# Attention and GraphSAGE of one kernel put into one fixed order, with common PSUM banks and tiles, and the first GraphSAGE batch prepared in the last attention steps

## The chip, the cores and the metric

The kernel runs on one core of a Trainium2 chip. Its engines run side by side: TensorE (PE, whose weight loads are listed apart as PEld), VectorE (DVE), ScalarE (ACT), GpSimd (POOL) and SyncE (SP), which here only issues transfers. A DMA transfer is started by an instruction on an engine's queue and lands on its own; the engines meet through semaphores. Times are device microseconds (us) of one execution. The time of the kernel before is the median of three runs, 3646.37 us (3645.41 to 3649.14).

## What is computed

Two graph layers over B = 16 graphs of N = 1024 nodes with D = 128 features and a dense adjacency with values 0 or 0.05 to 1. All data are float32.

```python
# layer 0: attention with H = 8 heads of 16
h = relu(layernorm(x))
q, k, v = (h @ W.T + b split into heads)
attn = softmax(where(adj == 0, -inf, q @ k.T / 4)) * adj
attn = attn / (attn.sum(-1) + 1e-8)
x = x + (attn @ v) @ Wo.T + bo

# layer 1: GraphSAGE on a thinned adjacency
h = relu(layernorm(x))
for n in range(1024):                  # one after the other, in each graph
    # of row n's remaining neighbours every sf-th is removed, from row and column
    sf = (num + 1) // 2 if num > 10 else 1
adj_d = adj * kept
for Wr, Wx, b, g, be in three layers:
    deg = max(adj_d.sum(-1), 1)
    out = (adj_d @ h) / deg @ Wr + h @ Wx + b
    h = batch_norm(relu(out / max(norm(out), 1e-12) * mask))   # statistics over all graphs and nodes
x = x + ((concat(h1, h2, h3) * mask) @ Wl + bl) * mask
```

## The kernel before

**Attention** is a chain of 512 half-steps: for each batch b (16), each half c of the 512 query rows (2), each block m of 128 keys (8), each group g of four heads (2). One half-step computes on PE the scores of four heads into two tiles `sc` (L459 puts a large negative number where there is no edge, L465 adds q times k), on ACT their exponentials `e` (L481), on DVE the product `w` with the transposed adjacency (L486), and on PE the sums over w and e into `acc` (L383, L388), one half-step later (`late`). Even half-steps also transpose a piece of the adjacency (L414) that ACT copies to `aT` (L417); that is stored to DRAM (`aT_d`) for GraphSAGE. L421 makes `nomask`, which also counts zeros.

Beside these steps run others, written as generators and taken on in a list `beside`. `go_on_with(kinds)` advances the first whose next part is of a wanted kind: True is a PE part, "evict" and "evict by VectorE" are the copies out of PSUM, False is work that needs neither. `prepare(b + 1)` makes q, k and v of the next batch, from `xt` with a layer norm (statistics on DVE, a power on POOL at L235, the normalisation on ACT at L241). `conclude` (L311 to L357) finishes a half of a batch: divide by the sums (L329 to L333, with a copy of the reciprocals to `rden` on POOL), transpose (L337), multiply by Wo (L347), add to x (L352); after the second half it also stores x (L355), makes the layer norm for GraphSAGE and stores its result `h0_d` (L357).

**The dilation** is a third generator, run beside attention by `beside_attention`: eight blocks of 128 rows over all 16 graphs, whose parts carry a cost, and which is advanced so that the sum of the costs keeps pace with the half-steps (`spent < total * (i + 16) / n_att`). It writes `mr_d`, nonzero where an edge was removed. Its last block ends shortly before attention does; two half-steps later the loads for GraphSAGE's first two turns are issued by `edges` (L122 to L131): the transposed adjacency of a half batch (2 MB) and two pieces of `mr` (512 KB each). Issued by name from ACT's queue, they stand among ACT's own instructions.

The order of PE, ACT and DVE in attention is the order of the code, since all of it is under `tc.manual_schedule`. The queues of SP and POOL are ordered by the scheduler of the tile framework.

**Between the two.** After the last half-step (L499) the second half of batch 15 is concluded, with nothing beside it. L826 to L843 add up what must hold for the sweep to be valid (`still`, `pf`, `bad`) into `flag`; a second form of the kernel, `walked`, runs if that is not zero, which it is not for these inputs. Then the masks of turn 0 are applied (L139: four pieces of 128 x 1024 per turn, an edge is dropped where mr is not zero); in the order that the scheduler builds, these and those of turn 1 stand on DVE among the last attention products. The attention pools, SBUF and PSUM, close here, and the pools const2, p2, p2small and p2ps take their memory: six weights, wl and bl (L857 to L862), norms, `ys` with a column of ones by memset (L877), rdeg, hTs.

**GraphSAGE** is 3 layers x 16 batches x 2 halves, 96 turns, again under `tc.manual_schedule`. Before each layer `incoming` and `given` prepare batch 0: in the first layer h0 is loaded (L931, from POOL's queue) and transposed (L939, L940), then multiplied by Wr into `ys` (L949, L950); a batch later on is prepared beside the one before. A turn (`nodes`) is: own = bias + h Wx (L105, L963), copied by ACT to `mine` (L966); sums over 8 x 4 blocks of the masked adjacency into `pg` (L971), in four parts with other work between them; degrees (L978, L981); o = pg / degree + mine (L985); its square (L990) and norm (L993 to L999), relu and scale (L1000); transposes (L1004), a copy into hTs (L1005) and statistics (L1007). The second part of one turn, from the square on, is run between the parts of the next turn's sums, as are the four mask pieces of the turn after. The adjacency is loaded three turns ahead, from SP's queue (`fetch`, L1012 to L1014). From the second layer on, `output_part` (L893) adds the layer's share of the output.

[...]Attention's tags are sc (2 tiles of 2 banks), acc0, acc1, m, d; GraphSAGE's are g (2 tiles of 2 banks), n, o, t, y.

Of the kernel before, what the change touches and what calls it, by code (L numbers as in the profile page):

```python
# [34 lines left out]
def swept(ctx: ExitStack, tc: tile.TileContext, t: dict, out: bass.AP, flag: bass.AP):  # L35
# [108 lines left out]

    ahead = {}

    with ExitStack() as p1:
# [3 lines left out]
        ps_s = p1.enter_context(tc.tile_pool(name="ps_s", bufs=2, space=PSUM))  # L151
        ps_o = p1.enter_context(tc.tile_pool(name="ps_o", bufs=1, space=PSUM))
        ps_m = p1.enter_context(tc.tile_pool(name="ps_m", bufs=1, space=PSUM))
        ps_d = p1.enter_context(tc.tile_pool(name="ps_d", bufs=1, space=PSUM))
# [3 lines left out]
        def load_x(b):  # L158
            if b < B:
                xts[b] = pool.tile([P, NB, D], F32, name=f"xt_{b}", tag="xin", bufs=3)  # L160
                nc.sync.dma_start(xts[b], x[b].rearrange("(k p) d -> p k d", p=P))
# [4 lines left out]
        nr_i = small.tile([B * NB, P], I32, name="nr_i", bufs=1)  # L166
        nc.sync.dma_start(nr_i, nodemask.rearrange("b (k p) -> (b k) p", p=P))
        nr_f = small.tile([B * NB, P], F32, name="nr_f", tag="raw", bufs=1)
# [3 lines left out]
        nc.vector.tensor_copy(mf, mps[:, : B * NB])  # L172
        nc.vector.tensor_scalar(
# [5 lines left out]
        raw = pool.tile([P, 4, D], F32, name="raw", tag="s", bufs=1)  # L179
# [39 lines left out]
        minus_half = one.tile([P, NB], F32, name="minus_half")  # L219
        nc.vector.memset(minus_half, -0.5)  # L220

        def layer_norm_relu(dst, src, name):

            st = small.tile([P, NB, 6], F32, name=f"st_{name}", tag="lnst", bufs=2)
            mv = small.tile([P, NB, 2], F32, name=f"mv_{name}", tag="lnmv", bufs=2)
# [7 lines left out]
            rs = small.tile([P, 2, NB], F32, name=f"rs_{name}", tag="lnrs", bufs=2)  # L233
# [11 lines left out]
        def prepare(b):  # L245
# [4 lines left out]
            h = pool.tile([P, NB, D], F32, name=f"h_{b}", tag="s", bufs=1)  # L250
            yield from layer_norm_relu(h, xt, f"a{b}")
            hT = one.tile([P, N], F32, name=f"hT_{b}", tag="hT")
# [105 lines left out]

        ready = {}
# [16 lines left out]
        def attention():  # L376
# [62 lines left out]
            for i, (b, c, m) in enumerate(turns):  # L439
                mm = slice(m * P, (m + 1) * P)  # L440
                if m == 0:
# [3 lines left out]
                    if c == 0 and b + 1 < B:  # L445
                        take_on(prepare(b + 1), len(beside))
                if c == 1 and m == HB + 1:
                    load_x(b + 2)
# [51 lines left out]
            take_on(conclude(*done), 0)  # L500
            while beside:
                go_on_with(True, False, "evict", "evict by VectorE", "first")
# [18 lines left out]
        def dilation():  # L521
# [23 lines left out]
            def fetch(k, b):  # L545

                ad = pool.tile([P, N], F32, name=f"ad_{k}_{b}", tag="ad", bufs=2)
# [1155 lines left out]
```

## Time and profile before

| | us |
|---|---|
| median of three runs (lowest, highest) | 3646.37 (3645.41, 3649.14) |
| the profiled execution's own time | 3647.81 |
| its span, first to last instruction | 3645.9 |
| PE busy | 3447.8 (95%) |
| DVE busy | 3161.1 (87%) |
| ACT busy | 2300.6 (63%) |
| POOL busy | 155.5 (4%) |
| PE, sums `pg` (L971) | 737.9, 6144 of 275 ns on average |
| PE, sums `acc` (L383 and L388) | 651.0 and 625.0, 4096 each |
| DVE, product `w` (L486) | 1204.3, 1024 of 1217 ns |
| DVE, masks (L139) | 458.8, 384 of 1217 ns |
| ACT, exponentials (L481) | 990.6, 1024 of 1020 ns |

The profile is of one execution. Busy times of an engine are shares of the whole span; a row of it cuts the span into 40 slices of 91 us with one digit each (tenths of the slice in which the engine was busy), and a row PEclk gives TensorE's granted clock in the same way. A window gives busy times in a stretch. In a timeline a line is: start (us from the start of the span), duration, engine, line of the code, operation, out<-in, shapes, how many were joined into the line, and in brackets how long the engine was idle before and what ended it. ACTq, SPq and POOLq are transfers issued on the queue of that engine. The chain of waits goes back from the last instruction to what released it.

### The profile page before, as it was taken

The page shows a single profiled execution, that of the slowest core. Times are in us where ns is not written, and L with a number is a line of the kernel's source. Part 1 is how long each engine was busy: PE and PEld are TensorE (multiplying, and loading weights), DVE is VectorE, ACT ScalarE, POOL GpSimd, SP SyncE. Part 2 cuts the span into 40 slices and gives each one's busy share as a digit, 9 for nine tenths or more (in the row PEclk, how much of TensorE's full clock was granted, in tenths as well). Part 3 has the DMA queues.
Part 4 walks back from the last instruction along what each step waited for, and adds up shares of the span by engine and source line. Part 5 has one row for each costly group of instructions (what it writes and reads, how often), then busy time and mean ns, then how long its engine had stood idle before and what let it go on. Part 6 is the DMA issues. An engine that isn't in the chain of part 4 may idle for free. (4 is left out here: it accounts for less than half of the span.)

```text
span 3645.9 us, 86038 instructions
## 1 busy us (share of the span) xinstructions
PE 3447.8 (95%) x34855; PEld 1895.4 (52%) x34855; DVE 3161.1 (87%) x5215; ACT 2300.6 (63%) x3813; POOL 155.5 (4%) x210
## 2 busy tenths in 40 slices
PE   6999999999999999999999999977999899989997
PEld 2333333333333333333333333326999799989996
DVE  3999999999989999999999999974788688878786
ACT  5689679779769869868967876852222333322224
POOL 1000000000000000000000000000000000000000
PEclk9999999999999999999999999988999999999999
DMA  6346447547637636736845853666999788889996
GB/s 189 112 143 198 148 118 215 150 124 217 179 110 212 200 115 199 222 109 184 238 138 151 233 169 109 188 208 225 329 331 318 257 318 314 317 298 333 332 332 197
DMA packets 654305, 772.77 MB, mean 212 GB/s; under 512 B 173765, under 2 KB 574026, under 8 KB 641610
## 3 DMA queue, kind: packets, MB, share of 16 engines
q1 hardware_dynamic: 639978, 718.95, 61.4%
q0 software_dynamic: 11520, 41.95, 3.3%
q8 instruction: 275, 4.51, 0.5%
q10 hardware_dynamic: 2400, 6.29, 0.5%
q14 instruction: 132, 1.08, 0.1%
HBM read 509.02 MB, written 157.29 MB: 183 GB/s over the span
## 5 line engine op out<-in xcount | busy, mean ns | idle before, releaser
L486 DVE TENSOR_TENSOR w<-e,aT 128x1024 f32<-128x1024 f32 x1024 | 1204.3, 1217 | 152.1 <-ACT e L481 151.3
L481 ACT ACTIVATE e<-sc 128x1024 f32<-128x1024 f32 x1024 | 990.6, 1020 | 427.0 <-PE sc L465 415.9
L971 PE MATMUL pg<-y,aT 128*128 128x128 f32 (+1 forms) x6144 | 737.9, 275 | 0.0
L971 PEld LDWEIGHTS pg<-y,aT 128*128 128x128 f32 x6144 | 712.2, 192 | 0.0
L383 PE MATMUL acc<-w,v_both 128*32 128x512 f32 x4096 | 651.0, 614 | 15.3 <-DVE w L486 11.4
L388 PE MATMUL acc<-e,eps 128*32 128x512 f32 x4096 | 625.0, 597 | 0.0
L465 PE MATMUL sc<-qT,kT 32*128 32x512 f32 x4096 | 593.2, 649 | 0.3 <-ACT qT L267 0.3
L139 DVE SCALAR_TENSOR_TENSOR aT<-mr,aT 128x1024 f32<-128x1024 bf16 x384 | 458.8, 1217 | 15.6 <-DMA mr<-mr_d 15.6
L388 PEld LDWEIGHTS acc<-e,eps 128*32 128x32 f32 x4096 | 159.0, 111 | 303.6 <-issue 295.6
L754 DVE TENSOR_TENSOR_SCAN wr<-rk 128x1024 f16<-128x1024 bf16 x128 | 291.7, 2279 | 0.0
L990 ACT ACTIVATE sq<-o 128x512 f32<-128x512 f32 x96 | 60.6, 631 | 361.6 <-DVE o L985 361.6
L459 PE MATMUL sc<-nomask,never 32*32 32x512 bf16 x8192 | 246.8, 387 | 35.3 <-ACT e L481 32.3
L459 PEld LDWEIGHTS <-never 32*32 32x32 bf16 x8192 | 78.2, 88 | 320.5 <-issue 299.2
L465 PEld LDWEIGHTS sc<-qT,kT 32*128 32x128 f32 x4096 | 161.8, 185 | 118.2 <-issue 117.4
L383 PEld LDWEIGHTS acc<-w,v_both 128*32 128x32 f32 x4096 | 100.8, 109 | 225.1 <-DVE w L486 123.1
L414 PEld LDWEIGHTS pa<-ident,a 128*128 128x128 f32 x1024 | 109.1, 142 | 197.9 <-issue 151.3
L1005 ACT COPY hT<-pt 128x512 f32<-128x512 f32 x96 | 56.2, 586 | 237.5 <-PE pt L1004 237.5
L767 ACT ACTIVATE wr<-wr,th 128x1024 f16<-128x1024 f16 x128 | 148.0, 1156 | 46.7 <-DVE wr L754 45.8
L414 PE MATMUL pa<-ident,a 128*128 128x128 f32 x1024 | 170.4, 290 | 3.3 <-DMA a<-in_adj 2.6
L421 ACT ACTIVATE nomask<-aT 128x512 bf16<-128x512 f32 x256 | 161.3, 630 | 8.1
L985 DVE SCALAR_TENSOR_TENSOR o<-pg,rdeg,mine 128x128 f32<-128x128 f32 x384 | 108.0, 344 | 61.0 <-PE pg L971 59.8
L417 ACT COPY aT<-pa 128x512 f32<-128x512 f32 x256 | 151.6, 592 | 12.2 <-PE pa L414 12.2
(206 smaller groups left out, 3933.3 us busy)
## 6 DMA issues: line engine op xcount, KB each, us to landing
aT<-aT_d SPq DMA_DIRECT2D x94, 2048.0 KB, 9.8
mr<-mr_d SPq DMA_DIRECT2D x188, 512.0 KB, 5.8
a<-in_adj SPq DMA_DIRECT2D x256, 256.0 KB, 4.0
aT_d<-aT SPq DMA_DIRECT2D x256, 256.0 KB, 4.2
ad<-in_adj SPq DMA_DIRECT2D x128, 512.0 KB, 4.3
nomask<-nomask SPq DMA_DIRECT2D x512, 96.0 KB, 2.3
nomask<-nomask SPq DMA_DIRECT2D x512, 64.0 KB, 2.6
nomask<-nomask SPq DMA_DIRECT2D x512, 32.0 KB, 2.5
```

What stands on the lines that cost most here:

```text
L139: nc.vector.scalar_tensor_tensor(part, mrs[h][:, j : j + 2, :].rearrange("p j n -> p (j n)"), 0.0, part, ALU.is_equal, ALU.mult)
L383: nc.tensor.matmul(acc[g][32 * j : 32 * j + 32, :], v1[:, m, 2 * j + g, :], ws[j // 2][:, j % 2, :], start=(m == 0), stop=False,)
L388: nc.tensor.matmul(acc[g][32 * j : 32 * j + 32, :], eps8, es[j // 2][:, j % 2, :], start=False, stop=(m == NB - 1),)
L414: nc.tensor.transpose(pa[:, k * P : (k + 1) * P], a[:, k, :], ident)
L417: nc.scalar.copy(aT[:, 0, :], pa)
L421: nc.scalar.activation(nomask[:, 0, :], aT[:, 0, :], AF.Relu, bias=1.0, scale=-1e38, accum_out=zeros[:, i : i + 1])
L459: nc.tensor.matmul(scs[j // 2][to : to + 32, j % 2, :], never[rows, rows], nomask[rows, j, :], start=True, stop=False, tile_position=(32 * ...
L465: nc.tensor.matmul(scs[j // 2][:, j % 2, :], kT[rows, mm], qTs[c][rows, g, :], start=False, stop=True, tile_position=(32 * j, 0),)
L481: nc.scalar.activation(e, scs[q], AF.Exp, scale=1.0 / math.sqrt(HD))
L486: nc.vector.tensor_tensor(w, es[q], aT.to_broadcast([P, 2, HN]), ALU.mult)
L754: nc.vector.tensor_tensor_scan(wrs[b], rk(b, 1, N + 1), rk(b, 2, N + 2), -1023.0, ALU.add, ALU.add)
L971: nc.tensor.matmul(pg[:, i // 2, at : at + width], aT[:, j, i * P : (i + 1) * P], y[:, j, :width], start=(j == 0), stop=(j == NB - 1),)
```

## The change

All of attention and GraphSAGE comes under one `tc.manual_schedule`, and what stood between them is spread over the steps at its two sides.

- *PSUM.* The pools ps_s, ps_o, ps_m, ps_d are opened once for the whole kernel. GraphSAGE's tags are put on attention's banks by `bank`: n on d, o on acc0, t on acc1, y on m, and pg on sc.
- *Tiles.* Tiles that both parts use move to the pool `shared`: three `xin` (attention's x; ys and the bias tile tb of GraphSAGE), two `s` (h and hT of attention; h0 and the output sums of GraphSAGE), two `ad` (the dilation's loads; GraphSAGE's h), gl and gm (the weights, four to a tile). tb is one tile instead of two buffers, and the setup's raw loads take the tags of q and k.
- *Batch 0 of GraphSAGE.* `begin_sage` is taken on beside attention in the last half of batch 15: it loads eight of the ten weights and h0 of batches 0 and 1 from POOL's queue, sets the ones in ys, transposes h0 of batch 0 and multiplies it by Wr through bank m.
- *Edges and masks.* `edges` of turns 0 and 1 are issued from POOL's queue instead of ACT's. The four mask pieces of turn 0 come in the last two half-steps, those of turn 1 in turn 0.
- *The conclusion of batch 15* is no longer run to its end after attention. It is handed over as `last_rows` and advanced one part at a time in turns 0 to 3.
- *The flag* (`judge`), the closing of the attention pools, and `move_in` (the pool p2, the load for turn 3, hTs, the last weights, norms, rdeg) follow the sums of turn 0; only then is turn 0's `own` copied to `mine`. Until that point loads go two turns ahead instead of three.

The steady turns of GraphSAGE and the half-steps of attention keep their code. The core of the diff ("..." stands for lines left out):

```diff
...
+    ps_s = ctx.enter_context(tc.tile_pool(name="ps_s", bufs=2, space=PSUM))
+    ps_o = ctx.enter_context(tc.tile_pool(name="ps_o", bufs=1, space=PSUM))
+    ps_m = ctx.enter_context(tc.tile_pool(name="ps_m", bufs=1, space=PSUM))
+    ps_d = ctx.enter_context(tc.tile_pool(name="ps_d", bufs=1, space=PSUM))
...
-    with ExitStack() as p1:
+    def first_part(p1):
...
-                xts[b] = pool.tile([P, NB, D], F32, name=f"xt_{b}", tag="xin", bufs=3)
+                xts[b] = shared.tile([P, NB, D], F32, name=f"xt_{b}", tag="xin", bufs=3)
...
-            h = pool.tile([P, NB, D], F32, name=f"h_{b}", tag="s", bufs=1)
+            h = shared.tile([P, NB, D], F32, name=f"h_{b}", tag="s", bufs=2)
...
-            hT = one.tile([P, N], F32, name=f"hT_{b}", tag="hT")
+            hT = shared.tile([P, N], F32, name=f"hT_{b}", tag="s", bufs=2)
...
+        def begin_sage():
+            yield False
+            load_weights(0)
+            load_weights(1)
+            yield False
+            fetch_h0(0)
+            fetch_h0(1)
+            for i in range(2):
+                ys.append(shared.tile([P, NB, D + 1], F32, name=f"y_{i}", tag="xin", bufs=3))
+                nc.gpsimd.memset(ys[i][:, :, D:], 1.0)
+            hT = shared.tile([P, N], F32, name="h_0_0", tag="ad", bufs=2)
+            ready["sage"] = hT
+            for what in (incoming_first, given):
+                for c in range(2):
+                    yield True
+                    yield from what(0, 0, c, hT, "y")
...
+                    if c == 1 and b + 1 == B:
+                        take_on(begin_sage(), len(beside))
...
-            take_on(conclude(*done), 0)
-            while beside:
-                go_on_with(True, False, "evict", "evict by VectorE", "first")
+            assert not beside
+            ready["last"] = conclude(*done)
...
-                ad = pool.tile([P, N], F32, name=f"ad_{k}_{b}", tag="ad", bufs=2)
+                ad = shared.tile([P, N], F32, name=f"ad_{k}_{b}", tag="ad", bufs=2)
...
-                    if i == ended + 2:
-                        for c in range(2):
-                            ahead[c] = edges(0, 0, c, nc.scalar, shared)
...
-        beside_attention()
...
-    const = ctx.enter_context(tc.tile_pool(name="const2", bufs=1))
-    pool = ctx.enter_context(tc.tile_pool(name="p2", bufs=2))
-    small = ctx.enter_context(tc.tile_pool(name="p2small", bufs=3))
-    ps = ctx.enter_context(tc.tile_pool(name="p2ps", bufs=1, space=PSUM))
...
+                if i == ended + 2:
+                    for c in range(2):
+                        ahead[c] = edges(0, 0, c, nc.gpsimd, shared)
+                if i + 2 >= n_att:
+                    pieces = masks(*ahead[0])
+                    for piece in pieces[:2] if i + 2 == n_att else pieces[2:]:
+                        piece()
+            for _ in todo:
+                pass
+            return ready["sage"], ready["last"]
...
+    banks = {"n": (ps_d, "d"), "o": (ps_o, "acc0"), "t": (ps_o, "acc1"), "y": (ps_m, "m")}
+    def bank(name, tag):
+        where, tag = banks[tag]
+        return where.tile([P, 512], F32, name=name, tag=tag)
...
+    places = [("Wr1", "Wx1", "Wr2", "Wx2"), ("Wr3", "Wx3", "Wl0", "Wl1"), ("Wl2", "bl")]
...
+    def load_weights(i):
+        w4 = shared.tile([P, 4, D], F32, name=f"weights_{i}", tag="gl" if i < 2 else "gm", bufs=2)
...
-        prev = pool.tile([P, NB, D], F32, name=f"acc_{L}_{b}", tag="acc")
+        prev = shared.tile([P, NB, D], F32, name=f"acc_{L}_{b}", tag="s", bufs=2)
...
-        tb = pool.tile([P, NB, D], F32, name=f"tb_{b}", tag="h0in")
+        if b == 0:
+            late["tb"] = shared.tile([P, NB, D], F32, name="tb", tag="xin", bufs=3)
+        tb = late["tb"]
...
-            h0s[b] = pool.tile([P, NB, D], F32, name=f"h0in_{b}", tag="h0in")
+            h0s[b] = shared.tile([P, NB, D], F32, name=f"h0in_{b}", tag="s", bufs=2)
...
+    def incoming_first(L, b, c, hT, tag="n"):
+        pt = bank(f"ht_{b}_{c}", tag)
+        for i in range(HB):
+            nc.tensor.transpose(pt[:, i * P : (i + 1) * P], h0s[b][:, c * HB + i, :], ident)
+        yield "evict"
+        nc.scalar.copy(hT[:, c * HN : (c + 1) * HN], pt)
...
-        mine = pool.tile([P, HB, D], F32, name=f"mine_{L}_{b}_{c}", tag="mine")
-        nc.scalar.copy(mine, own)
-        pg = ps.tile([P, 2, 512], F32, name=f"pg_{L}_{b}_{c}", tag="g", bufs=2)
+        def evict():
+            mine = late["pool"].tile([P, HB, D], F32, name=f"mine_{L}_{b}_{c}", tag="mine")
+            nc.scalar.copy(mine, own)
+            return mine
+        mine = evict() if late else None
+        pg = ps_s.tile([P, 2, 512], F32, name=f"pg_{L}_{b}_{c}", tag="sc")
...
+        if not mine:
+            mine = evict()
+            yield "mine"
+        pool, small, rdeg = late["pool"], late["small"], late["rdeg"]
...
+    def move_in():
+        late["pool"] = ctx.enter_context(tc.tile_pool(name="p2", bufs=2))
+        fetch(3)
+        for b in range(B):
+            hTs.append(late["pool"].tile([P, N], F32, name=f"hT{b}", bufs=1))
+        late["small"] = ctx.enter_context(tc.tile_pool(name="p2small", bufs=3))
+        load_weights(2)
+        for i in range(3):
+            nc.gpsimd.dma_start(norms[:, i, 0:1], t[f"L1_gnn_g{i + 1}"].rearrange("(d o) -> d o", o=1))
+            nc.gpsimd.dma_start(norms[:, i, 1:2], t[f"L1_gnn_be{i + 1}"].rearrange("(d o) -> d o", o=1))
+        late["rdeg"] = late["small"].tile([P, B * NB], F32, name="rdeg", bufs=1)
...
+        hT, last_rows = attend()
+        next(last_rows)
...
+                    for n in range(i, i + 4 if late else i + 3):
...
+                    if i == 0:
+                        next(last_rows)
...
+                    if i < 4:
+                        next(last_rows, None)
...
+                    if i < 4:
+                        next(last_rows, None)
+                        if i == 0:
+                            next(last_rows)
...
+                    if i == 0:
+                        next(last_rows)
+                        judge()
+                        p1.close()
+                        move_in()
+                        new_stats(0)
+                        go(this, "mine")
...
```

## The prediction

> **What bounds the kernel now.** I read the busy shares first (PE 95%, DVE 87% of the span), then the row of TensorE's clock, which dips in only one place before the last slice, and cut that place up by windows. Columns: stretch, length, busy us of PE, PEld, DVE, ACT, POOL, granted clock, DMA share, GB/s.
>
> ```profile
> 2000.00:2426.00 426.00, 415.98 (x4570) 150.98 (x4567) 406.62 (x586) 332.04 (x477) 16.20 (x17) 0.99 0.59 176
> 2426.00:2471.50 45.50, 27.48 (x237) 6.97 (x238) 23.57 (x21) 13.41 (x16) 0.00 (x0) 0.77 0.57 202
> 2471.50:2515.50 44.00, 22.97 (x136) 19.91 (x136) 7.73 (x35) 8.94 (x18) 5.58 (x11) 0.65 0.57 206
> 2515.50:2847.00 331.50, 320.49 (x2737) 308.10 (x2737) 264.65 (x515) 95.17 (x188) 6.45 (x12) 0.99 0.91 321
> ```
>
> Attention (up to 2426) is held by PE and DVE together, 98% and 95% busy; GraphSAGE's first layer by PE, 97%. Between them lie 89.5 us in which nobody is full. The timeline shows two separate stalls there. The first is inside attention:
>
> ```profile
> 2426.02 1.94 ACT L481 ACTIVATE e<-sc 128x1024 f32<-128x1024 f32 x2 [1.56 <-PE sc L465]
> ...
> 2428.48 0.36 ACTq L126 DMA_DIRECT2D aT<-aT_d  x1
> ...
> 2434.61 2.82 ACTq L130 DMA_DIRECT2D mr<-mr_d  x2
> 2437.47 0.52 ACTq L126 DMA_DIRECT2D aT<-aT_d  x1
> 2438.03 1.05 ACTq L130 DMA_DIRECT2D mr<-mr_d  x2
> 2439.12 1.94 ACT L481 ACTIVATE e<-sc 128x1024 f32<-128x1024 f32 x2 [9.93 <-DMA mr<-mr_d]
> ...
> 2450.00 1.23 DVE L139 SCALAR_TENSOR_TENSOR aT<-mr,aT 128x1024 f32<-128x1024 bf16 x1 [6.04 <-DMA mr<-mr_d]
> 2451.14 2.35 DVE L486 TENSOR_TENSOR w<-e,aT 128x1024 f32<-128x1024 f32 x2
> ```
>
> The six loads for GraphSAGE's first two turns stand in ACT's own queue. In the order of the built program the second mask load shares a completion counter with the 2 MB load and waits until that lands (2437), so the exp of half-step 507 comes 13.1 us after that of 506, where undisturbed ones are 3.5 apart. Then DVE, whose order has a mask piece of turn 1 ahead of the attention product L486, waits for its load until 2450. The last product with the values ends at 2471.5. The second stall is the handover:
>
> ```profile
> 2483.72 3.18 ACT L241 ACTIVATE xt<-xt,rs_b 128x128 f32<-128x128 f32 x8 [7.77 <-DVE rs_b L237]
> 2486.93 0.32 SPq L357 DMA_DIRECT2D h_d<-xt  x1
> 2489.58 0.33 SPq L859 DMA_DIRECT2D Wr<-in_L_gnn_Wr  x1
> ...
> 2490.44 1.27 POOL L931 DMA_DIRECT2D h0in<-h_d  x2 [0.43 <-issue]
> ...
> 2494.92 1.09 PE L939 MATMUL ht<-ident,h0in 128*128 128x128 f32 x4 [14.32 <-DMA h0in<-h_d]
> ...
> 2515.52 0.38 PE L105 MATMUL own<-bias,ones 3*128 3x512 bf16 x1
> ```
>
> Conclusion and layer norm of batch 15, store, release of the attention pools, weights, h0 of batch 0, its transposes and products: one chain. 2515.52 starts turn 1, and from there PE keeps 20.75 us per batch without a gap (L963 at 2526.18, 2546.94, 2567.69). I compare the time at which turn 1 starts.
>
> **Part 1: attention's tail.** The new order issues those six loads from POOL, where each stands as early as its buffer allows: four masks and h0 about batch 14's end, the first 2 MB between the rden casts that lie at 2333 and 2342 now, the second after block 7's last batch (2410 now). ACT keeps no load. DVE masks turn 0 in half-steps 510 and 511, turn 1 after attention. Added on PE in 505 to 511: eight transposes and eight Wr products, at the warm rows 2 x 0.66 + 2 x 1.06 = 3.4 us; 0.66 of them falls before exp 506, already. From exp 506: one interval with its four transposes 3.88 (504 to 505), four of 3.5 (505 to 506, 2462.60 to 2466.11), plus 2.4 of added PE work (the last product hides in the wait for w, but I count 0.66 + 0.66 + 1.06): 20.3 to exp 511. From exp 511 to the end of values 5.4 (2466.11 to 2471.5), plus 1.35, because two mask pieces (2 x 1.22) put w of 511 past the 1.05 at which it begins now. So 2426.0 + 27.0 = 2453.1, against 2471.5: **18.4 gained**. ACT's four added copies (0.59) lie beside: ACT is 78% busy there.
>
> **Part 2: the handover.** Weights, h0, transposes and products of batch 0 are done by then; the conclusion is fed into turns 0 to 3. PE's turn 0 in the new order, warm rows: own 0.38 + 1.16, h0 transposes 0.66 x 2, conclusion's transposes 0.66 x 3, its product 0.37 + 1.16, Wr product 1.06, sums 4 x 1.95: 15.3 us gaps included. DVE's order: conclusion pairs (0.26 + 0.42) x 2, four mask pieces 4.9, in time for PE; then xt's add (0.69) when the product ends at 12.3, and the flag's reductions L826 to L836: 0.29 + 0.68 + 1.22 + 0.08 + 0.15 + 0.16 + 0.42 + 0.41 = 3.4, with gaps 3.9. This is a new wait: "mine" (ACT, 0.59) goes into the memory of the closed pools and in the built order waits for L836; queued behind it on PE is turn 1's own, which needs the same bank. 12.3 + 0.8 + 3.9 + 0.7 = 17.7 us from the end of values to turn 1, where it is 2515.5 - 2471.5 = 44.0 now: **26.3 gained**. Without that wait it would be 15.3.
>
> **Part 3: what it costs later.** The rest of the conclusion's layer norm (four times 0.78, and 0.34) falls to DVE in turn 1, where DVE is 8.4 of 10.4 us busy and begins late, at 18.1, when the flag is done (L836 at 17.0, two small operations, pf 0.56 on PE, two more). Its queue from there: degrees 0.34, o 1.13, two parts of the norm 1.56, mask 1.22, norm of o 0.85, mask 1.22, factor 0.33, o 0.69: o of turn 0 is ready at 25.7 with gaps; PE asks at 17.7 + 1.5 + 1.1 + 3.9 = 24.2: 1.5 late, and 0.4 again in turn 2, after which DVE's spare 2 us a turn catches up: **1.9 lost** (0 to 5). ACT's eight norms (3.4) fit: ACT is under 4 of 10 us there. SP's queue: the load of turn 3 waits for the pools' release at 16.7, behind turn 4's; both are 2 MB, 4 MB at the 339 GB/s of the window 2525.90:2536.20 are 12 us, and masks are wanted a turn later: no stall. SP also loses its 14 small loads in front of them. The single tb is rewritten once a batch, some 20 us after it was read: nothing. The common banks are as many as before, one tag each: nothing, and the last rival prices it.
>
> **Part 4: the start.** xt's buffer now lies where the setup pool was, so batch 0's x load waits for the third bias store. At present x is issued at 2.30, DVE reads it at 6.50, and h begins at 16.84. The third bias store: pieces at 3.32, DVE 0.48 + 0.81 + 0.21 + 0.48 + 0.79 + 0.47, so issue about 7.6, landing about 2 us later (nearest row: small setup loads), x issued 9.7, landed 13.7, statistics 3.2, POOL's pow 1.66 and the ends: h at 19.1. **2.3 lost** (0 to 4), and attention, always full, cannot win it back. The norms' small loads move to POOL, idle.
>
> [...] The nearest row: h0's loads from POOL take 0.54 us of issue beside a DVE 80% busy, and pow takes 1.64 in some rows and 3.45 in others beside attention. [...]
>
> [...] Now four transposes take 1.09 at 2494.92 and 0.66 at 2521.70, with the clock at 0.65 in the handover. [...] Should the granted clock fall to half, turn 0's rows cost about 11 us more.
>
> **Sum.** 18.4 + 26.3 - 1.9 - 2.3 = 40.5. The profiled execution took 3647.81 for a span of 3645.9; it becomes 3605.4 and 3607.3. The median of the runs is 3646.37, 1.4 lower: 3605.9, say **3606**.
>
> **The rivals.**
> - *The stall comes back at DVE:* POOL's loads land after the first mask is wanted (2444), and attention waits as now. For it: both stalls now end on these loads. Against: they issue 30 to 100 us ahead. Only parts 2 to 4 remain: 40.5 - 18.4 = 22.1, 3624. Chance 0.07.
> - *Turn 0 is slow:* cold PE, or DVE falls further behind. For it: DVE has nearly 12 us of 17.7 in that turn, in a chain with PE. 40.5 - 11 = 29.5, 3617. Chance 0.13.
> - *More is gained:* the start costs nothing, no lag, the flag hidden (17.7 to 15.3): 47, 3599. Chance 0.12.
> - *No change:* the moved work only displaces work of equal length. Against: the windows hold 39 us of PE time without work. Chance 0.02.
> - *Slower:* GraphSAGE's steady turns suffer from the common tiles and banks (h shares attention's two buffers, h0 and acc share one pair). 96 turns: from 0.42 us a turn on the gain is gone. Against: the orders of PE, DVE and ACT in those turns are unchanged, each bank still has one tag. With 0.55 us a turn it would be 3605.9 + 96 x 0.55 = 3659. Chance 0.04.
>
> **How the numbers follow.** The forecast has 0.62, its own range 3600 to 3613 (start +-2, lag 0 to 5, tail +-3). The range 3597 to 3619 adds the larger gain and the slow turn 0, leaving out the returning stall, no change, slower, and edges: about 0.18. Within 0.2% (7.3 us) is what a measurement of this kernel can hardly tell from none: same 0.02, slower 0.04, faster 0.94.
>
> **What would show it.** Right: exp intervals of 3.5 to 4.6 to the end, no L126 in ACT's queue, no DVE wait for mr in attention (part 1); first pg about 3 us after the last acc, turn 1's own 17 to 18 us after it, with ACT's mine ended by DVE's L836 (line numbers moved) (part 2); PE waiting for o once or twice under 2 us (part 3); first exp near 35.5 instead of 33.2 (part 4). Wrong: POOL's loads holding back rden or pow and DVE behind them; a clock under 0.9 between 2430 and 2480; a first-layer batch longer than 20.75.

## The result and the profile after

The changed kernel takes 3612.10 us (median of four runs, 3607.07 to 3615.53) where the kernel before takes 3647.76 (the three runs of the table ahead and a fourth, 3645.41 to 3651.41): a ratio of 0.9897 with a 95% interval of 0.9883 to 0.991, 33 to 43 us or 0.9 to 1.2% off. The forecast was 3606, with a range of 3597 to 3619 and an own range of 3600 to 3613. The direction, the size and most of the steps were right; the median lies 6 us above the point. A second trace of the changed kernel, of an execution of 3612.82 us, shows where such a difference lies: of its 5.7 us over the first trace 4.7 are there by exp 506, in the start and in attention, which the forecast had left as it was, and none in the steps around the handover.

The profiled execution is the fastest of the four: 3607.07 us for a span of 3605.3. Against the span before, 3645.9, it gains 40.6 us. Cut at the same events as the prediction:

| stretch | before, us | after, us | measured gain | predicted |
|---|---|---|---|---|
| start to exp 506, the start in it | 2426.02 | 2431.41 | -5.4 | -2.3 |
| exp 506 to the last product with the values (tail) | 45.47 | 25.55 | 19.9 | 18.4 |
| from there to turn 1's own (handover) | 44.03 | 15.13 | 28.9 | 26.3 |
| turn 1 to turn 4 | 31.10 | 34.88 | -3.8 | -1.9 |
| turn 4 to the end | 1099.28 | 1098.33 | 0.95 | 0 |
| sum | 3645.9 | 3605.3 | 40.6 | 40.5 |

The sum fits better than its parts deserve, and that is luck: the two large gains came out 4.1 above the forecast, the two losses 5.0 above it. The 0.95 at the end is no gain: the same stretch took 1098.6 us in a second trace of the kernel before and 1099.3 in the second of the changed one.

The windows of the profile after, with the columns as in the prediction; the cuts are the end of attention's undisturbed part, the last product with the values and turn 1's own.

```profile
2000.00:2431.40 431.40, 421.22 (x4640) 152.56 (x4633) 412.95 (x593) 339.39 (x488) 27.20 (x37) 1.00 0.65 196
2431.40:2457.00 25.60, 25.05 (x257) 8.22 (x257) 18.34 (x16) 14.86 (x19) 0.53 (x1) 1.00 0.25 78
2457.00:2472.05 15.05, 13.25 (x112) 12.53 (x111) 10.16 (x20) 3.51 (x6) 0.93 (x3) 1.00 0.95 332
2472.05:2803.55 331.50, 321.40 (x2736) 309.05 (x2736) 264.60 (x529) 96.42 (x193) 9.12 (x15) 0.99 0.93 331
```

The second and third rows were 89.5 us with a clock of 0.77 and 0.65. Now they are 40.7 us, PE is busy for 25.05 of 25.60 and 13.25 of 15.05, and the clock is 1.00. GraphSAGE's first layer is full as before.

In attention's tail the timeline of ACT shows exps without a stop, and nothing of the loads in its queue:

```profile
2431.41 1.94 ACT L510 ACTIVATE e<-sc 128x1024 f32<-128x1024 f32 x2 [1.46 <-PE sc L494]
...
2435.28 1.94 ACT L510 ACTIVATE e<-sc 128x1024 f32<-128x1024 f32 x2 [0.70 <-PE sc L494]
...
2442.66 1.94 ACT L510 ACTIVATE e<-sc 128x1024 f32<-128x1024 f32 x2 [1.56 <-PE sc L494]
2444.49 0.59 ACT L984 COPY y<-pn 128x512 f32<-128x512 f32 x1
2447.04 1.94 ACT L510 ACTIVATE e<-sc 128x1024 f32<-128x1024 f32 x2 [1.96 <-PE sc L494]
```

Turn 0 and turn 1 on PE (the timeline, transposes and products of the conclusion among GraphSAGE's sums), and the copy of `own` to `mine` on ACT:

```profile
2456.90 0.38 PE L105 MATMUL own<-bias,ones 3*128 3x512 bf16 x1
...
2459.08 1.95 PE L1011 MATMUL pg<-y,aT 128*128 128x129 f32 x16
...
2466.16 1.16 PE L356 MATMUL pr<-attn_w,cxT 128*128 128x128 f32 x8
2467.16 1.06 PE L982 MATMUL pn<-weights,h 128*128 128x128 f32 x8
2468.05 1.95 PE L1011 MATMUL pg<-y,aT 128*128 128x129 f32 x16
2471.35 0.58 ACT L1002 COPY mine<-own 128x512 f32<-128x512 f32 x1 [2.51 <-DVE still L866]
2471.80 0.35 PE L870 MATMUL pf<-still,ones 128*128 128x2 f32 x2 [1.80 <-DVE still L868]
2472.09 0.38 PE L105 MATMUL own<-bias,ones 3*128 3x512 bf16 x1
...
2474.29 3.74 PE L1011 MATMUL pg<-y,aT 128*128 128x129 f32 x32
2480.37 0.63 PE L1048 MATMUL pt<-ident,o 128*128 128x128 f32 x4 [2.35 <-issue]
2480.84 5.38 PE L1011 MATMUL pg<-y,aT 128*128 128x129 f32 x32
2486.15 0.39 PE L105 MATMUL own<-bias,ones 3*128 3x512 bf16 x1
```

Two waits are left. At 2471.80 PE has waited 1.80 us for the flag's reductions on DVE, and so has ACT's `mine` (L866 is the reduction of `zeros`, L836 in the kernel before). At 2480.37 it has waited 2.35 us in front of the transposes of o (the program has them wait for o of turn 0, which DVE finishes at 2480.27), and the 32 sums behind that gap take 5.38 us, where 32 took 3.74 just before.

### The profile page after: what moved, and what is told of

It is laid out like the page before. It is cut to its first block, busy times and chain, and to the rows that moved or that the text cites. A ratio compares the mean times of both kernels' runs of the same rounds, so it can differ in the third digit from the quotient of the medians.

```text
span 3605.3 us, 86057 instructions
## 1 busy us (share of the span) xinstructions
PE 3437.5 (95%) x34855; PEld 1889.5 (52%) x34855; DVE 3159.5 (88%) x5215; ACT 2300.5 (64%) x3813; POOL 168.2 (5%) x232
## 4 chain that ended last, share of the span: by engine, by line
PE 44%; DVE 41%; ACT 6%; DMA 5%; issue 3%; SPq 2%; ACTq 0%; POOL 0%; DVEq 0%; POOLq 0%
DVE w L515 15%; PE pg L1011 14%; PE sc L494 6%; PE acc L410 5%; PE acc L415 4%; DVE wr L782 4%; DVE hit L717 3%; DVE aT L139 3%; ACT e L510 3%; PE pn L982 2%; PE sc L488 2%; PE own L997 2%; DMA nomask<-nomask 2%; PE pt L1048 2%; DVE o L1029 1%
```

## The experiments

One row for each kernel, from its profile (us): its attention body (exp 0 to exp 506), the tail, the handover and turns 1 to 4 as in the table above, and its median with the ratio to the kernel before that ran beside it. The medians of the kernel before differ from one set of runs to the next (3647.76 to 3656.99), so medians of different sets are compared by their ratios.

| kernel | body | tail | handover | turns 1 to 4 | median | ratio (95%) |
|---|---|---|---|---|---|---|
| before (profiled twice) | 2392.8, 2394.7 | 45.5, 45.6 | 44.0, 43.8 | 31.1 | | |
| changed, again | 2399.3 | 25.6 | 15.1 | 34.9 | 3615.24 | 0.9904 (0.9888 to 0.9921) |
| late flag | 2400.7 | 25.6 | 13.0 | 32.9 | 3608.93 | 0.9883 (0.9867 to 0.9900) |
| early x | 2406.5 | 25.6 | 15.1 | 34.9 | 3613.11 | 0.9891 (0.9875 to 0.9908) |
| late flag, early x | 2398.0 | 25.6 | 13.0 | 32.9 | 3606.36 | 0.9878 (0.9861 to 0.9894) |
| the same, layer norm later | 2401.3 | 25.6 | 13.0 | 31.4 | 3612.17 | 0.9896 (0.9881 to 0.9912) |
| edges on ACT | 2398.1 | 38.7 | 15.1 | 34.7 | 3633.56 | 0.9938 (0.9918 to 0.9958) |
| batch 0 not ahead | 2404.0 | 24.3 | 21.9 | 33.6 | 3622.03 | 0.9902 (0.9881 to 0.9924) |
| conclusion first | 2397.5 | 25.6 | 25.1 | 32.0 | 3619.26 | 0.9900 (0.9878 to 0.9923) |
| both, only the loads ahead | 2397.8 | 24.3 | 34.3 | 32.0 | 3634.31 | 0.9939 (0.9919 to 0.9959) |
| before, edges on POOL | 2420.8 | 23.3 | 42.7 | 31.1 | 3649.83 | 0.9994 (0.9983 to 1.0004) |
| before, edges on POOL, masks placed | 2397.8 | 24.3 | 47.2 | 31.1 | 3633.83 | 0.9954 (0.9940 to 0.9967) |

The tail, the handover and the turns repeat within 0.3 us from one kernel to the next wherever their code is the same; the body scatters by 10 us and more. So these three are read from the traces, where a median could not tell 4 us.

### The first stall: queue and place

One part undone, the loads from ACT's queue again:

```diff
-                        ahead[c] = edges(0, 0, c, nc.gpsimd, shared)
+                        ahead[c] = edges(0, 0, c, nc.scalar, shared)
```

> One part undone: the loads for turns 0 and 1 are issued from ACT's queue again, at the same step; the masks stay in the last two half-steps and in turn 0. Theory (the queue makes the first stall): exp 507 follows exp 506 after over 12 us instead of 3.9, because the loads in ACT's queue wait for their counters and buffers, and DVE waits again for mr ahead of the first mask; attention ends 9 to 16 us later, 3619 to 3626. Rival (the stall came from eight mask pieces of DVE in attention's tail, which are now four): ACT loses only the issue time of six loads, under 4 us.

Exp 507 follows exp 506 after 15.36 us and the tail grows by 13.2, in the middle of what the theory gave; the rest is as in the changed kernel. The traced execution (3624.61) lies in the range given, the median (3633.56) over 7 us above it, in a set in which the kernel before too was slow (3656.99); that difference was not traced. The timeline of this kernel has ACT's stall of before again, but not DVE's: the masks, which have their place here, do not wait for mr, where the theory had them wait.

```profile
2437.89 0.36 ACTq L126 DMA_DIRECT2D aT<-aT_d  x1
...
2444.97 3.28 ACTq L130 DMA_DIRECT2D mr<-mr_d  x2
2449.36 0.34 ACTq L126 DMA_DIRECT2D aT<-aT_d  x1
2449.78 0.96 ACTq L130 DMA_DIRECT2D mr<-mr_d  x2
2450.79 1.94 ACT L510 ACTIVATE e<-sc 128x1024 f32<-128x1024 f32 x2 [12.18 <-DMA mr<-mr_d]
```

Then the same part alone, in the kernel before:

```diff
-                            ahead[c] = edges(0, 0, c, nc.scalar, shared)
+                            ahead[c] = edges(0, 0, c, nc.gpsimd, shared)
```

> One part alone: the kernel before with nothing changed but the queue of the loads for turns 0 and 1, POOL in place of ACT. Theory (the queue makes the first stall): exp intervals of 3.5 to 4.7 to the end, no wait of DVE for mr; exp 506 to the last product with the values 26 to 31 us instead of 45.5 (all eight mask pieces still stand in attention's tail, which is worth 0 to 5 us), the handover 44 as before; 3631 where the kernel before has 3647 to 3650. Rival: the loads are the bound, and what attention's tail wins the handover gives back, under 4 us in all. Its attention body, exp 0 to exp 506, is that of the kernel before, and a second sample of it: 2393 again if the body of the changed kernel (2395 to 2407, nine executions) is really slower, 2395 to 2405 if 2392.8 was a lucky execution.

It gains nothing: 0.9994. The tail is 22 us shorter, somewhat more than the theory said, but the body is 26 to 28 longer. Exp 505 now comes 15.42 us after exp 504 (3.88 in the kernel before), and the slice of half-steps 488 to 496 takes 49.3 us instead of 40.3; these two make 20.5 of the 26 to 28, and the rest lies ahead of exp 440, in the body's scatter. The timeline names both places, DVE's masks of turn 0 and, after POOL's load, those of turn 1:

```profile
2354.06 2.36 DVE L139 SCALAR_TENSOR_TENSOR aT<-mr,aT 128x1024 f32<-128x1024 bf16 x2 [4.65 <-DMA aT<-aT_d]
...
2426.86 0.60 POOL L126 DMA_DIRECT2D aT<-aT_d  x1 [11.36 <-DVE er L774]
...
2437.53 4.63 DVE L139 SCALAR_TENSOR_TENSOR aT<-mr,aT 128x1024 f32<-128x1024 bf16 x4 [7.91 <-DMA aT<-aT_d]
```

The masks of the kernel before have no place of their own in attention's order. With the loads on another queue the built order puts turn 0's four pieces at half-steps 487 and 488 and turn 1's at half-step 503, under 3 us after their 2 MB were issued; DVE stands 4.7 us for the first load and 7.9 for the second, with attention's products and the dilation's last steps queued behind. Neither theory had this: the expectation counted the masks at 0 to 5 us where they stood. What moved the loads forward moved their users forward too, to a place where DVE had no room.

So the part was tried alone with both its halves, the masks of turn 0 in the last two half-steps and those of turn 1 after attention:

```diff
+                        ahead[c] = edges(0, 0, c, nc.gpsimd, shared)
+                    if i + 2 >= n_att:
+                        pieces = masks(*ahead[0])
+                        for piece in pieces[:2] if i + 2 == n_att else pieces[2:]:
+                            piece()
...
+                for piece in masks(*ahead[1]):
+                    piece()
...
-    for piece in masks(*ahead[0]):
-        piece()
...
```

> One part alone, now with both halves of it: the kernel before, the loads for turns 0 and 1 on POOL's queue, and the masks of turn 0 written into the last two half-steps, those of turn 1 after attention, where the queue alone had left their place on DVE to the scheduler (which put turn 1's four masks 7.9 us ahead of their transfer, in the middle of the dilation's last steps). Theory (the first stall is queue and place together): half-steps of 3.5 to 4.7 to the end, exp 506 to the last product with the values 24 to 27 us instead of 45.5, the handover 44 as before: 19 to 21 us off, a ratio of 0.994 to 0.995. Rival (what the tail wins, the later loads and the handover give back, as with the queue alone): within 4 us of the kernel before. Its attention body is a fourth sample of the kernel before, 2393 to 2396 if that body is really shorter than the changed kernel's (2395 to 2407).

Tail 24.3, as expected; 0.9954, 17 us instead of the 19 to 21, because the handover is 3.1 longer. Turn 1's four masks do not lengthen it on DVE: ACT ends the layer norm 15.6 us after the last product (15.4 in the kernel before). What comes later are the loads behind it. The store of h0 now stands in SP's queue between two mask loads, whose buffers these masks set free:

```profile
2470.21 0.37 SPq L130 DMA_DIRECT2D mr<-mr_d  x1
2471.16 0.32 SPq L357 DMA_DIRECT2D h_d<-xt  x1
2472.49 0.37 SPq L130 DMA_DIRECT2D mr<-mr_d  x1
2475.83 0.33 SPq L863 DMA_DIRECT2D Wr<-in_L_gnn_Wr  x1
```

In the chain of waits it takes 4.53 us where it took 2.57, and h0's load, issued 0.3 us later after the landing than before, takes 4.7 instead of 4.2; whether the mask loads beside it are the cause no run here shows, since none takes them away. The first stall is the queue and the place together, and nearly half of the whole change is to be had without any of the rest.

### The handover: what of it is loads, what is order

```diff
-                    if c == 1 and b + 1 == B:
-                        take_on(begin_sage(), len(beside))
...
             assert not beside
+            whole(begin_sage())
```

> One part undone: the transposes and Wr products of batch 0 come after attention instead of beside its last half-steps, one after the other through one bank; the loads of weights and of h0 still go out early. Theory: the last half-steps shorten by 2.4 us, and the handover grows by four rounds of PE and ACT (2 x (0.66 + 0.59) + 2 x (1.06 + 0.59), with their gaps about 7): 4 to 5 us more in all. Rival: the handover had room for them, under 1 us.

The tail is 1.25 shorter (not 2.4: the part that counted was 0.38 and 0.88, and the last product had been lying in PE's wait for w), the handover 6.8 longer, turns 1 to 4 1.3 shorter: 4.3 in all, as expected.

```diff
         hT, last_rows = attend()
-        next(last_rows)
+        whole(last_rows)
+        last_rows = iter([0] * 40)
```

> One part undone: the conclusion of batch 15, its layer norm with it, runs to its end before turn 0. Theory: its chain of 15.4 us (last values to the end of the layer norm on ACT, before the change) stands in front of the copies that turn 0 needs from ACT, so the way from the last values to turn 1 grows from 15.2 to about 24, and 3.7 us of that come back in turn 1, where DVE no longer has the statistics: 4 to 6 us more. Rival: turn 0's sums do not need ACT and hide the conclusion, under 1 us.

The handover grows by 9.9, of which 2.9 come back in turns 1 to 4: 7.0, a little above the 4 to 6. Both at once:

> Both of the last two undone: conclusion, then transposes and products of batch 0, then turn 0, with only the loads ahead. Theory: 15.4 for the conclusion, 7 for batch 0, 12 to 15 for turn 0: last values to turn 1 34 to 37 us, against 44 before the change and 15.2 after, so of the 28.8 us won there some 8 to 10 belong to the loads being early and the rest to work put beside other work; the time is 13 us over the changed kernel, less or more by 3. Rival (the loads were the whole stall): within 5 us of the changed kernel.

34.3 us, within the theory's 34 to 37, and in all 15.0 more than the changed kernel over tail, handover and turns. Of the 28.9 us of the handover 9.8 (44.0 to 34.3) are thus won without laying any work beside turn 0. 8.0 of them are the way from the end of the layer norm to batch 0's first transposes in the kernel before (2486.90 to 2494.92: store, release, loads), which is gone here: the first of them run before the layer norm does, since their tiles do not wait for attention's memory. The other 19.1 are work laid beside other work, with PE's clock in it: 0.70 on average over this run's handover, 1.00 in the changed kernel's. The rival, that the loads were the whole stall, falls.

### The flag and the rest of the lag

```diff
-        signs = one.tile([P, NB, 2, B], F32, name="signs")
+        signs = const.tile([P, NB, 2, B], F32, name="signs")
...
                         next(last_rows)
-                        judge()
                         p1.close()
...
+                    if i == 8:
+                        flag_steps = judge()
+                    if 8 <= i < 16:
+                        next(flag_steps, None)
```

(zeros, rden and changed likewise; judge becomes a generator in six parts, and its tile fits is bf16 in place of float32.)

> The flag's reductions are spread over turns 8 to 15, and what they read stays in memory that is not given up; turn 0's mine no longer waits for them. Theory (the flag stands in a chain): PE's wait of 1.8 us ahead of pf and of turn 1's own goes, DVE starts turn 0's o about 2.2 us earlier, and turn 2 follows turn 1 after 11 to 12 us instead of 14.1. The span from the last values to turn 2's own falls from 29.25 to 23.5 to 26, so 3 to 6 us off the time against the changed kernel beside it. Rival (DVE is full in these turns by the layer norm of batch 15 anyhow): only the place of the wait moves, under 1.5 us.

PE's wait in front of turn 1 is gone (handover 12.97) and turn 2 follows after 11.58 instead of 14.06; over turns 0 to 4 45.9 us instead of 50.1, and 0.23 are lost once in turn 12, which now holds the flag's product on PE (0.28). 4.0 us, within the theory; the rival falls.

> The setup of the biases uses three of the mask buffers in place of a pool of its own whose memory x's buffer takes over, so the load of x for batch 0 stands sixth in SP's queue again. Theory: first exp at 33.2 instead of 36.1, but at half-step 16 only about 1 us of the 2.95 is left, since the first half-steps wait for loads that did not move (before against after, the lag was 2.95 at half-step 0, 0.69 at half-step 6, 1.04 at 16); the time falls by 1, which the runs can hardly show. Rival, as the prediction had it: attention is full, the whole 2.95 stays.

The edit: the pool of the biases' setup goes, and its three tiles are taken from the buffers of the masks.

```diff
-    with tc.tile_pool(name="setup", bufs=1) as where:
-        vecs = where.tile([1, 2, n, D], F32, name="vecs")
+    shared = ctx.enter_context(tc.tile_pool(name="shared", bufs=1))
+    setup = [shared.tile([P, HB * HN], BF, name=f"setup_{i}", tag="mr", bufs=4) for i in range(3)]
...
```

The first exp comes at 34.34, 2.5 earlier than in the changed kernel beside it (36.85) but 1.1 later than before, not at 33.2 as expected: ACT's first two copies of the adjacency stand in front of h, and the transposes that they wait for begin at 13.52 us instead of 12.68, behind DVE's copy of the transposed weights. At half-step 16, over all profiles, the seven kernels with the late load are at 128.3 to 131.0 us (mean 129.8), the three with the early one at 126.8 to 127.6 (127.1), the four of the kernel before and its variants at 126.5 to 127.2 (126.7). So the late x costs about 3 us, and at half-step 16 they are still there: the theory of 1 rested on one execution (128.28 against 127.24), and the rival holds. What half-step 16 gains is lost in the body's scatter by the end (this execution had the longest body of all the changed kernels, 2406.5), so the median, 2.1 lower, says little.

> Both of the above in one kernel. Theory: the gains add, 1 at the start and 3 to 6 at the handover: 4 to 7 us under the changed kernel beside it, so about 3604 where that is 3610. Rival: under 2 us in all, because a DVE that is full in turns 1 to 3 takes the handover's part back.

3606.36, 8.9 under the changed kernel measured beside it (0.9878 against 0.9904, intervals that just overlap), where 4 to 7 were expected; the traces account for 4.0 at the handover and 2.5 at the first exp (34.32 for 36.85), and the rest is within the scatter.

> The kernel with late flag and early x, and besides the layer norm of batch 15 taken one part per turn from turn 3 on instead of four per turn in turns 1 to 3. Theory: DVE has 3.4 us less in turns 1 and 2, so turn 2 follows turn 1 after 10.4 instead of 11.57 and turn 3 turn 2 after 10.8 instead of 11.36: 1.7 us, all of the handover's lag gone, about 1 to 2 us under that kernel, where runs can hardly show it but the turns do. Rival: the lag comes from o of turn 0, which waits for mine, and stays at 11.5.

```diff
-                    if i < 4:
-                        next(last_rows, None)
+                    if i == 0:
+                        next(last_rows)
...
+                    elif i > 2:
+                        next(last_rows, None)
```

Turn 2 follows after 10.59 and turn 3 after 10.83 (10.35 and 10.82 before the change): the lag was DVE's, and it is gone but for 0.24 us. The median, 3612.17 beside a kernel before of 3650.74, does not show these 1.5 us; the body of its profiled execution was 3.3 us longer than that of the kernel without the edit, which is more than they are.

### Attention's body

> The changed kernel once more, unaltered, as the yardstick for the runs beside it. Theory: the handover is fixed by its order, so from the last product with the values to turn 1's own it takes 15.2 us again and turn 2 starts 14.1 us after turn 1, while attention's body (exp 0 to exp 506: 2395.3 in the profiled execution, 2392.8 before the change) differs from one execution to the next by some us, at places that differ. Rival: the body's extra 2.4 us belong to the change; then it is 2395 again with the late half-steps at the same places (128, 147, 209, 338, 392). Median 3607 to 3614.

> The kernel before, unaltered, for a third sample of attention's body. In nine executions of changed kernels the slices of eight half-steps agree within 0.2 us with each other and with the kernel before, except where the granted clock dips (0.96 or 0.92 in a slice, some 1.6 us each) near the ends of the dilation's blocks, and at half-steps 120 to 136, where a wait for a shifted copy of nomask comes and goes. Theory (both are chance): the kernel before shows them too, and its body scatters over 2393 to 2405. Rival (the moved tiles or queues cause them): 2392 to 2394 again.

The body of the changed kernel was 2399.3 in this execution, not 2395.3, with its delays at other half-steps. Cut into slices of eight half-steps, the executions agree within 0.2 us in most slices and differ in a few, near the ends of the dilation's blocks. One of them, half-steps 384 to 392, in the kernel before, the changed kernel and the kernel with early x (windows; the last three figures are clock, DMA share, GB/s):

```profile
1847.69:1885.53 37.84, 36.13 (x412) 12.93 (x413) 37.36 (x76) 24.61 (x37) 3.91 (x3) 1.00 0.33 101
```

```profile
1853.25:1892.67 39.42, 37.72 (x412) 13.40 (x413) 38.56 (x76) 24.60 (x37) 3.91 (x3) 0.96 0.32 97
```

```profile
1861.26:1901.93 40.67, 38.95 (x412) 13.66 (x413) 38.60 (x76) 24.62 (x37) 3.91 (x3) 0.92 0.32 96
```

The same instructions, and in all three the same gap of PE before one product of the dilation:

```profile
1878.83 0.55 PE L697 MATMUL gone<-one_bf,hit 128*128 128x1 bf16 x16 [1.52 <-DVE hit L689]
```

```profile
1884.39 0.55 PE L725 MATMUL gone<-one_bf,hit 128*128 128x1 bf16 x16 [1.52 <-DVE hit L717]
```

After it eight products of w with the values take 1.07 us in the kernel before and 1.94 in the changed one. At a clock of 0.96 this slice took 39.3 to 39.5 us in three executions, 1.4 to 1.6 more than at 1.00. Over all slices of half-steps 16 to 496, in thirteen executions, one with a clock of 0.94 to 0.97 was 0.0 to 1.65 us longer than the same slice at 1.00, with a median of 1.0. Over half-steps 16 to 440 the clock records of the 14 traces hold the clock at half for 8 to 17 stretches of 3.41 us, and the time grows with their number, by about 1.4 us for each (a fit; 8 and 1993.9 us in the kernel before, 17 and 2009.8 in the one with early x). The scatter of the body is for a good part this. The kernel before has such dips too (half-steps 16, 88, 136, 200, 448 among others), so the change is not what causes them. Its body in this second sample, 2394.7, is itself no proof of scatter: the expectation's rival gave 2392 to 2394, its theory 2393 to 2405.

Whether the body is longer with the change is less clear. From exp 0 to exp 440, ahead of everything that was moved at its end, it took 2088.0, 2089.7, 2095.2 and 2094.5 us in the four profiles of the kernel before and its two variants (mean 2091.9), and 2091.9 to 2103.1 in ten of the changed kernel and its variants (mean 2095.6): 3.7 us between the means, with ranges that overlap. The fourth of the first group, the kernel before with queue and place, was expected at a body of 2393 to 2396 if that kernel's is really shorter; it took 2397.8. The stretch of half-steps 118 to 136 differs most steadily, 82.3 to 84.0 against 83.7 to 86.3. PE waits there for shifted copies of nomask (2.3 to 4.0 us between half-steps 110 and 140 in the first group, 2.3 to 5.2 in the second, products and weight loads together). Whether these land later with the change, and why, was not tried and stays open.

## Why the prediction was right, and where not

**Part 1** (18.4 predicted, 19.9 measured). The exps came at 3.5 to 4.4 us, no load in ACT's queue, no wait of DVE for a mask. The added PE work was counted too high: four transposes of h0 cost 0.38 (half-steps of 3.88 for 3.50) instead of 0.66, the first Wr product 0.88 instead of 1.06. The prediction gave the masks their place in its sum, but counted the gain as the queue's: the queue alone brings nothing (3649.83), and the rival that the stall comes back at DVE, given 0.07, is what happens when the masks are not given their place. It did not come true because the change places them.

**Part 2** (26.3, 28.9). The chain was as described, down to mine waiting for the reduction of zeros on DVE (the line at 2471.35 above). The term that was too large is the time to the end of the conclusion's product: 12.3 us after the values in the sum, 10.4 in the trace, since four groups of sums and the pieces between them follow each other at their starts, 1.79 us for 16 sums where the row of 1.95 counts the overlap with the next group twice. Without the wait it would be 13.0, not 15.3: the run with the late flag.

**Part 3** (1.9, 3.8). PE waited for o once, as said, but 2.35 us instead of 1.5. Of the difference 0.48 is a wait of DVE that its queue in the prediction did not have, for ACT's factor, with a table load in front of it:

```profile
2477.64 1.28 ACT L1040 ACT_TABLE_LOAD   x1 [1.58 <-DVE f L1039]
2479.17 0.18 DVE L1042 RECIPROCAL f<-f 128x4 f32<-128x4 f32 x1 [0.48 <-ACT f L1040]
```

And the 32 sums behind the wait took 5.38, 1.64 more than the 32 in front of it. The clock says why (windows of the changed kernel, the 32 sums in front of the wait and the 32 behind it):

```profile
2474.30:2478.00 3.70, 3.70 (x34) 3.53 (x32) 3.67 (x13) 1.95 (x4) 0.00 (x0) 1.00 0.99 425
2480.84:2486.10 5.26, 5.26 (x34) 5.18 (x32) 3.67 (x9) 0.59 (x1) 1.41 (x1) 0.68 0.75 249
```

The sum had priced a wait at its own length; here PE paid for it again at a clock of 0.68. SP's queue, the single tb and the common banks cost nothing, as argued: from turn 4 on the starts of the first layer's turns keep their distance to those of the kernel before within 0.1 us, and at the last of the 96 it is 0.5 us shorter, so the rival of slower turns has no ground.

**Part 4** (2.3, 2.95 at the first exp). The stations were met within 1.1 us: x issued at 10.20 for 9.7, read at 14.81 for 13.7, h at 19.47 for 19.1. Over seven executions the first exp comes 3.6 us later than in four of the kernel before (36.9 for 33.3), and about 3 are left at half-step 16, so attention indeed does not win it back, as far as the scatter lets one follow it; the size was 1.3 too small.

**The loads from POOL, and the clock of turn 0.** The six loads from POOL took 0.54 to 0.80 us of issue each beside a DVE that is 96% busy in that stretch (179.8 of the 187 us from 2229 to 2416), and the mask pieces landed 4.9 to 8.3 us after, the two 2 MB loads 9.5 and 10.4. Whether DVE's work lengthens an issue or a landing no run here shows. Turn 0 ran on warm rows, 0.60 for four transposes, at a granted clock of 1.00. That the sum could take these rows, its gaps of up to 2.4 us included, was the author's assumption: no run shows a length up to which a gap leaves the clock alone. In this trace the clock stayed at 1.00 over the gap of 1.80 us at the end of turn 0 and was 0.50 for 3.41 us after the one of 2.35 in turn 1; that a gap costs only its own length, as the sum took it, was the weak half (below).

**The point and the median.** By its own trace the changed kernel would have been at 3607.07, one microsecond from the forecast; its median is 5 us above that, and the repetition beside its own kernel before gained 36.8 us, the first set 35.7, where 40.5 were forecast. The term that was off is the one left out: attention's body as a constant. On average the seven changed kernels with the late x reach exp 440 6.6 us later than the four of the kernel before (2131.8 for 2125.2), 3.6 of it at the first exp and 3.0 between, while the stretches behind gain 45.0 (19.9 + 28.9 - 3.8): 38.4 by this count. The profiled execution lay at the short end of that scatter, and a range with a body of plus or minus 5 us around the same sum would have said the same thing better.

## What to carry to other kernels

When a load is moved to an earlier queue, ask where its consumer stands: an instruction whose place is left to a scheduler follows its data forward, and can stop a full engine there that had nothing to do with the old stall. Give both their places by hand, or neither. In a handover between two stages, count the loads apart from the order: here tiles that need not wait for the first stage's memory brought a third, and work of the second stage laid beside the first the rest. Put reductions that nobody waits for behind the handover, not into it.

## What the runs showed of the hardware

In these traces the granted clock of PE is not decided by the program alone. A gap of 1.52 us (1.53 in the third) in front of the same sixteen small products was followed by a full clock in one execution, a dip to 0.96 of the slice in another and to 0.92 in the third. A slice's figure is an average: in narrow windows of the changed kernel the clock is 1.00 ahead of the wait for o, 0.50 for one stretch of 3.41 us behind it and 1.00 again, and the dip of half-steps 384 to 392 (last line) is such a stretch too:

```profile
2475.60:2477.90 2.30, 2.30 (x22) 2.23 (x20) 2.27 (x5) 0.72 (x2) 0.00 (x0) 1.00 1.03 442
2480.97:2484.38 3.41, 3.41 (x19) 3.41 (x18) 3.38 (x8) 0.59 (x1) 0.00 (x0) 0.50 0.67 223
2484.40:2487.80 3.40, 3.40 (x29) 3.05 (x29) 1.62 (x9) 0.00 (x0) 1.66 (x1) 1.00 0.83 217
1887.06:1890.46 3.40, 3.40 (x20) 1.31 (x20) 2.92 (x10) 2.70 (x4) 0.20 (x1) 0.50 0.03 7
```

3.41 us at half the clock are, as an estimate, 1.7 us of work lost; the sums behind o took 1.64 more, and the slice of half-steps 384 to 392 with one dip 1.4 to 1.6.

At one place, in front of o's transposes in turn 1, gaps of 2.15 to 2.35 us were followed by slow sums in each of four executions (5.36 to 5.38 us for the 32 behind them), and gaps of 0.5 to 1.5 us in six others were not (3.74, as with the late flag):

```profile
2482.46 0.63 PE L1053 MATMUL pt<-ident,o 128*128 128x128 f32 x4 [1.51 <-issue]
2482.92 3.74 PE L1016 MATMUL pg<-y,aT 128*128 128x129 f32 x32
```

The 1.52 us of attention's gap lie between the two and were followed by either; what decides it no run here shows.
